# Layer 3's serial taps on the raw image, with scale and mean folded into the pointwise weights

## The chip, the core and the metric

The kernel runs as one program on one core of a Trainium2 chip. The metric is the time of one execution on the device in microseconds (us); the median of three runs before the change is 26167.87 us (26167.0 to 26171.33). The engines are called as in the profile: PE multiplies matrices, DVE works on vectors, ACT evaluates functions and scaled copies, POOL is a second vector engine, SP issues most transfers (DMA). Each engine works through its own queue in order.

## The reference, cut to what matters

The input x is 16 images of 192 channels and 64 x 64 points. Four layers follow one another, each of the form x = x + layer(group_norm(x)). The change concerns the last, and its group norm:

```python
# --- layer 3 --- (B, C, H, W) = (16, 192, 64, 64)
def _gn(v, G=32, eps=1e-5):            # groups of 6 channels
    g = v.reshape(B_, G, C_ // G, H_, W_)
    m = jnp.mean(g, axis=(2, 3, 4), keepdims=True)
    s = jnp.var(g, axis=(2, 3, 4), keepdims=True)
    return ((g - m) / jnp.sqrt(s + eps)).reshape(v.shape)

def _L3_conv_ref(x, w3, w5, wh, wv, pw, gamma, beta):   # x is already _gn(x)
    y = _dwconv(x, w3, 1) + _dwconv(x, w5, 2) + _dwconv(x, wh, (0, 3)) + _dwconv(x, wv, (3, 0))
    z = jnp.einsum('oc,bchw->bohw', pw, y)
    zn = (z - mean(z)) * jax.lax.rsqrt(var(z) + BN_EPS)     # over all images
    return jnp.clip(gamma * zn + beta, 0.0, 6.0)
x = x + _L3_conv_ref(_gn(x), ...)
```

The four depthwise convolutions (3x3, 5x5, 1x7 and 7x1, all with zeros outside the image) are one sum of 29 taps: the 25 points of the 5x5 square, the two ends of the 1x7 row and the two ends of the 7x1 column.

## The kernel before, in words

Two images make a pair: 384 channels, held as three tiles of 128 partitions (j = 0, 1, 2). There are 8 pairs, and `pair` runs for each the function `scans` and then `layer3`.

**scans** is layer 2 (a state-space scan) of the pair, 768 steps. Beside it runs a generator `fr` (`stream`), of which a few items are issued per scan step: layers 0 and 1 of the next pair, and at the end `ahead`, the depthwise convolution of layer 3 for tile j = 0 of the present pair. `ahead` works in 8 units of 512 points: 20 taps on PE (`a_p <- a_x,diag`), 6 on ACT and POOL (`a_g`, `a_m`), 3 on DVE; the sum is copied by ACT (`a_y`) and stored in `y0_d` by SP. The order of all engines is that of the program text (`keep_in_program_order`). At the end of `scans` (lines 1360 to 1365) the last four sums are added up on PE, `finish` takes the statistics of the last rows of the tile `X` (tile j = 2 of the layer's input, 70 x 70 with a border of zeros) and stores them, and what is left of `fr` is drained. In the last pair there is no next pair, and `fr` is done long before.

**layer3** (line 1513) convolves the tiles j = 1 (`xp1`, in the profile `xp`, loaded from `x3_d`) and j = 2 (`X`, still in place). It first asks on SP for `xp1`, the diagonal weights `diag`, the pointwise weights `pw` (they lie in a part of `Xt`), parts of `y0_d`, and `xn`, the first tile of the next pair's scan. Then it runs `group_norm` (means over partitions by small matmuls with `grp` into `gn_sum`), normalises both tiles in place on DVE (line 1544), in two parts, first the upper 19 rows, and `xn` too (line 1549). Then come 8 units u: four chunks c of 16 rows, each for j = 1 and 2. The 29 taps of a unit are shared out by the list `TAPS`: the first 7 go to PE (`products`, matmuls with diagonal weights into `l_p`), the next 9 to ACT, which multiplies, and POOL, which adds (`side`, tiles `l_g` and `l_m`), the other 13 to DVE. `add_side(u - 1)` adds `l_g` into `l_p` on PE; DVE then does the last tap of unit u - 1, which also writes the result (`l_y`, or a part of `Xt`), and twelve of unit u (`vector`). From u = 3 on the pointwise product `z` of a finished chunk is made on PE (`z_pe`), copied by ACT (`z_act`), its statistics taken by DVE (`z_dve`). The last chunk's `z` is made in the next pair's scans (`last_z`).

The queue order of one round u, which decides who waits for whom, is:

```python
products(u, 0)                  # 1654
products(u, 1)
add_side(u - 1)
...
last_tap(u - 1)                 # 1668
vector(u)
z_dve()
```

The program records most instructions from the helper at line 71, so that line stands beside nearly all of them, and tiles have to be told apart by name.

Of the kernel before, what the change touches and what calls it, by code (L numbers as in the profile page):

```python
# [11 lines left out]
F32 = mybir.dt.float32  # L12
# [10 lines left out]
P = 128  # L23
# [22 lines left out]

TAPS = [(3, 0), (3, 6), (0, 3), (6, 3)] + [(y, x) for y in range(1, 6) for x in range(1, 6)]
PE_TAPS = 7  # L50
GP_TAPS = 9


VECTOR_CHUNKS = 9
# [58 lines left out]
def conv_preact_kernel(ctx: ExitStack, tc: tile.TileContext, a: dict):  # L113
# [49 lines left out]
    dsk = load("dsk", [P, K, NT])  # L163
    b1c = load("b1c", [P, NT])
    wc = const.tile([P, NT, 7, 7], F32, name="wc")
    one_c = const.tile([P, 1], F32, name="one_c")
    minus_c = const.tile([P, 1], F32, name="minus_c")
    nc.vector.memset(one_c, 1.0)
# [72 lines left out]
    with tc.tile_pool(name="prep", bufs=1) as prep, tc.tile_pool(  # L241
# [118 lines left out]
        for part, w in (  # L360
            (wc[:, :, 2:5, 2:5], w3x3),
            (wc[:, :, 3, :], w1x7),
            (wc[:, :, :, 3], w7x1),
        ):
            nc.vector.tensor_tensor(part, part, w, ALU.add)
        for j in range(NT):
            diag = prep.tile([P, AHEAD_PE, P], F32, name="diag", tag="diag", bufs=1)
            many = PE_TAPS if j else AHEAD_PE
            for t, (ty, tx) in enumerate(TAPS[:many]):
                nc.gpsimd.tensor_scalar(  # L370
                    diag[:, t, :], ident, wc[:, j, ty, tx : tx + 1], None, ALU.mult
                )
            nc.sync.dma_start(out=diag_d[:, j, :many, :], in_=diag[:, :many, :])
# [44 lines left out]
    def normalise(eng, o, v, gm, rstd, j):  # L418
        eng.tensor_scalar(o, v, gm[:, j : j + 1], rstd[:, j : j + 1], ALU.subtract, ALU.mult)
# [668 lines left out]
        E.gps.tensor_tensor(image(du), image(delta), columns(xn)[:, : LC // HW, :], ALU.mult)  # L1088
        return xn, bp, delta, du

    def scans(i, o, p3, st3, begun, nxt, closing):

        E = _Engines(tc, True)
        with ExitStack() as es:
# [264 lines left out]
                    add_up(s - LATE)  # L1359
            for s in range(total - LATE, total):  # L1360
                add_up(s)
            for g in (finish(NT - 1, todo[-1][2] // LC), fr):
                for _ in g:
                    E.between()
            E.between()

    def ahead(i, E, ps, less, rstd):
# [89 lines left out]
    def end_z(E, i):  # L1457

        for j in range(NT):
            E.dve.bn_aggr(zmv[:, j, :], zst[:, j, :, :].rearrange("p c s -> p (c s)"))  # L1460
        E.sp.dma_start(out=zstat_d[i], in_=zmv.rearrange("p j s -> p (j s)"))
# [15 lines left out]
    def last_z(i):  # L1477

        def run(E, ps, pool):
            c = HW // 16 - 1  # L1480
            held, stats = None, []
            for jo in range(NT):
                for h in range(2):
                    for call in stats:
                        E.later(call)
                    stats.clear()
                    if held is not None:
                        held()
                    p = ps("cz_p")
                    z_product(E, p, jo, h, kept)  # L1490

                    def held(jo=jo, h=h, p=p):
                        z = pool.tile([P, 512], F32, name="cz", tag="cz", bufs=2)
                        E.act.copy(z, p)
                        stats.append(lambda: E.dve.bn_stats(zst[:, jo, 2 * c + h, :], z))
                        at = 1024 * c + 512 * h
                        E.sp.dma_start(out=row_tiles(z_d[i])[:, jo, at : at + 512], in_=z)

                    yield
            for call in stats:  # L1500
                E.later(call)
            stats.clear()
            held()
            yield
            for call in stats:
                E.later(call)
            yield
            E.later(lambda: end_z(E, i))
            yield

        return run

    def layer3(i, st3, o_next):
        E = _Engines(tc, True)
        units = [(c, j) for c in range(4) for j in range(1, NT)]
        own = PE_TAPS + GP_TAPS

        with tc.tile_pool(name="l3s", bufs=1) as stat, tc.tile_pool(name="l3y", bufs=2) as yk, tc.tile_pool(
            name="l3z", bufs=3
# [13 lines left out]
            E.sp.dma_start(out=xp1, in_=x3_d[i, 1])  # L1533
            E.sp.dma_start(out=diag, in_=diag_d[:, 1:, :PE_TAPS, :])
            E.sp.dma_start(out=pw, in_=a["pw"])
            for c in (0, 1, 3):
                load_y0(c)
            loaded = load_first(E, o_next) if o_next is not None else None
            xps = {1: xp1, 2: X}
            gm = stat.tile([P, NT], F32, name="gm")  # L1540
            rstd = stat.tile([P, NT], F32, name="rstd")
            for _ in group_norm(E, st3, stat, banks, gm, rstd, aside=False):
                pass
            for rows in (slice(3, 22), slice(22, 3 + HW)):
                for j in (1, 2):
                    v = xps[j][:, rows, inside]
                    normalise(E.dve, v, v, gm, rstd, j)
            if o_next is not None:
                normalise(E.dve, loaded[0], loaded[0], o_next.gm, o_next.rstd, 0)

            def window(j, c, rows, tap):
                return xps[j][:, c + tap[0] : c + tap[0] + rows, tap[1] : tap[1] + HW]
# [4 lines left out]
            def side(u, taps):  # L1557
                if u < len(units):
                    c, j = units[u]
                    for n in taps:  # L1560
                        tap = TAPS[PE_TAPS + n]
                        if n == 0:
                            m = gs[u] = wk.tile([P, 1024], F32, name="l3_g")
                        else:
                            m = wk.tile([P, 1024], F32, name="l3_m", bufs=3)
                        E.act.activation(
                            image(m), window(j, 16 * c, 16, tap), AF.Copy, scale=factor(j, tap)
                        )
                        if n:
                            E.gps.tensor_tensor(gs[u], gs[u], m, ALU.add)  # L1570

            def products(u, h):
                if u < len(units):
                    c, j = units[u]
                    if h == 0:
                        pss[u] = pt.tile([P, 1024], F32, name="l3_p")
                    cs = slice(512 * h, 512 * h + 512)
                    for t, tap in enumerate(TAPS[:PE_TAPS]):
                        E.pe.matmul(
                            pss[u][:, cs],  # L1580
                            diag[:, j - 1, t, :],
                            window(j, 16 * c + 8 * h, 8, tap),
                            start=(t == 0),
                            stop=(t == PE_TAPS - 1),
                        )

            def add_side(u):
# [21 lines left out]

            def vector(u):  # L1610
                if u < len(units):
                    for tap in TAPS[own:-1]:
                        tap_on_vector(u, tap, pss[u])

            def last_tap(u):
# [10 lines left out]
            def z_act(key):  # L1626
                c, jo, h = key
                if h == 0:
                    zs[c, jo] = zk.tile([P, 1024], F32, name="z")
                E.act.copy(zs[c, jo][:, 512 * h : 512 * h + 512], zps.pop(key))  # L1630
                stats.append(key)

            def z_dve():
# [8 lines left out]
            rounds = len(units) + (1 if o_next is not None else 3)  # L1642
            late, begun = [], None
            for u in range(rounds):
                c = (u - 3) // 2
                todo = [(c,) + x for x in halves[3 * ((u - 3) % 2) :][:3]] if u >= 3 else []
                side(u, range(0, 2))
                for key in late[:1]:
                    z_act(key)
                side(u, range(2, 4))  # L1650
                for key in late[1:]:
                    z_act(key)
                late = []
                products(u, 0)
                products(u, 1)
                add_side(u - 1)
                for key in todo[:2]:
                    z_pe(*key)
                side(u, range(4, 7))
                if todo:  # L1660
                    z_act(todo[0])
                side(u, range(7, GP_TAPS))
                if todo:
                    z_pe(*todo[2])
                    late = todo[1:]
                if u == 5 and o_next is not None:
                    begun = begin(E, o_next, loaded, lambda: pt.tile([P, 1024], F32, name="l3_p"))
                last_tap(u - 1)
                vector(u)
                z_dve()  # L1670
                if u == 4:
                    load_y0(2)
# [2 lines left out]
            z_dve()  # L1675
            if o_next is None:
                end_z(E, i)
            return begun

    def pair(i, q, more, begun, closing):  # L1680

        with tc.tile_pool(name="st3", bufs=1) as p3:
            st3 = p3.tile([P, NT, 8, 6], F32, name="st3")
            nxt = None if more is None else (more, sets[1 - q])
            scans(i, sets[q], p3, st3, begun, nxt, closing)
            if more is not None:
                return layer3(i, st3, sets[1 - q])
            with tc.tile_pool(name="zl", bufs=2) as pool:
                got = [load_z(u, pool) for u in range(3)]
                layer3(i, st3, None)  # L1690
                final(got, pool)

    def load_z(u, pool):
# [196 lines left out]
```

## Time and profile before

| what | value |
|---|---|
| median of 3 runs | 26167.87 us |
| time of the profiled execution | 26165.92 us |
| its span, first to last instruction | 26164.1 us |
| mean granted PE clock | 0.954 |
| DVE, 12 taps of a unit (`l_p<-X,wc,l_p`) | 15.86 us |
| POOL, mean of one add `l_g<-l_g,l_m` | 2406 ns |
| stretch 3965.2 to 4022.4 (first pair: end of the scans to the first DVE tap of layer 3) | DVE busy 19.69 of 57.20 us, PE 47.47, ACT 15.18, POOL 22.74 |
| stretch 4022.4 to 4190.0 (the rest of layer 3) | DVE busy 142.78 of 167.60 us, PE 144.33, ACT 82.24, POOL 143.64 |

A line of the timeline reads: start in us from the beginning of the span, length in us, engine, line of the program, operation, output <- inputs, shapes, count; and in brackets the time that the engine had been idle before, and what ended it. A matmul in f32 appears as two records, here called passes. A line of the table of groups ends in the busy time, the mean of one in ns, and the idle time before, with what ended it.

### The profile page before, as it was taken

The numbers are of one execution on the slowest core, as the hardware profiler recorded it, in microseconds if no ns is written. First come the engines' busy times: TensorE is split into PE (matmuls) and PEld (weight loads), VectorE is DVE, ScalarE is ACT, GpSimd is POOL, SyncE is SP. The second block draws the span as 40 slices with busy tenths as digits, with TensorE's granted clock in tenths as the row PEclk, the third lists the DMA queues.
The fourth block names the chain that finished last, engine by engine and source line by source line (L and its number), as shares of the span: only waits on it lengthen the run. The fifth ranks groups of instructions, "written<-read, shape, count | busy, mean of one in ns | idle before, by whom it ended". The sixth has DMA issues, their size and how long they took to land. (4 is left out here: it accounts for less than half of the span.)

```text
span 26164.1 us, 211030 instructions
## 1 busy us (share of the span) xinstructions
PE 23141.7 (88%) x58228; PEld 9496.0 (36%) x58228; DVE 23813.2 (91%) x15461; ACT 16268.9 (62%) x23559; POOL 20558.9 (79%) x10503
## 2 busy tenths in 40 slices
PE   7899989999899988999889998999989998866773
PEld 3344333433334333443334433343333433322231
DVE  7499998999899998999989999899989999899995
ACT  7388456874578655885558845687457865444443
POOL 3388877887788877888778887788778887777773
PEclk9899999999999999999999999999999999988896
DMA  3589875898678975899758987589867997567766
GB/s 84 155 227 229 222 227 169 228 225 223 196 200 230 227 221 168 225 233 225 223 167 228 227 223 226 169 229 226 223 189 205 229 227 222 160 187 193 196 200 270
DMA packets 2025599, 5449.12 MB, mean 208 GB/s; under 512 B 552616, under 2 KB 552840, under 8 KB 2007904
## 3 DMA queue, kind: packets, MB, share of 16 engines
q1 hardware_dynamic: 1799776, 4575.16, 60.2%
q0 software_dynamic: 221184, 805.40, 16.2%
q10 hardware_dynamic: 3456, 55.05, 0.5%
q8 instruction: 465, 7.62, 0.1%
q14 instruction: 718, 5.88, 0.1%
HBM read 3887.10 MB, written 358.39 MB: 162 GB/s over the span
## 5 line engine op out<-in xcount | busy, mean ns | idle before, releaser
L71 POOL TENSOR_TENSOR h<-h,cb 128x1024 f32<-128x1024 f32 x6144 | 14910.2, 2488 | 3330.5 <-ACT state L71 2798.7
L71 DVE TENSOR_TENSOR_SCAN h<-dA,state,pbt 128x1024 f32<-128x1024 f32 x4608 | 10806.5, 2345 | 541.9 <-ACT dA L71 91.4
L71 PE MATMUL ysum<-h,ident 128*128 128x512 f32 x18432 | 9050.3, 615 | 113.8 <-DMA h<-h 108.6
L71 DVE TENSOR_TENSOR pbt<-du,pbt 128x1024 f32<-128x1024 f32 x6144 | 7429.4, 1209 | 289.8 <-PE pbt L71 268.4
L71 ACT ACTIVATE dA<-delta,t_alog 128x1024 f32<-128x1024 f32 x6144 | 7036.6, 1146 | 6.6
L71 PEld LDWEIGHTS ysum<-h,ident 128*128 128x128 f32 x18432 | 3612.2, 197 | 4321.7 <-issue 3909.2
L71 ACT COPY state<-h 128x1 f32<-128x1 f32 x6144 | 1143.0, 186 | 5828.6 <-DVE h L71 5811.2
L71 DVE TENSOR_TENSOR_SCAN h<-dA,pbt 128x1024 f32<-128x1024 f32 x1536 | 3509.2, 2285 | 179.6 <-ACT dA L71 26.6
L71 PE MATMUL pbt<-bp,pick 96*128 96x512 bf16 x8192 | 2549.0, 394 | 1220.1 <-DVE h L71 1211.6
L71 PE MATMUL p<-m,wms 128*96 128x512 f32 (+1 forms) x5376 | 2664.7, 597 | 59.4 <-ACT lu L71 35.3
L71 PEld LDWEIGHTS <-pick 96*128 96x128 bf16 x8192 | 691.6, 100 | 4013.6 <-DVE h L71 2468.2
L71 PE MATMUL l_p<-l_xp,w1s 128*128 128x512 f32 x3920 | 1850.0, 593 | 0.0
L71 POOL DMA_DIRECT2D h<-h x1536 | 1356.2, 883 | 496.6 <-POOL h L71 427.0
L71 PE MATMUL pbt<-bp,pick_mix 96*128 96x512 bf16 x4096 | 1270.9, 392 | 516.7 <-DVE h L71 514.9
L71 ACT ACT_TABLE_LOAD x1103 | 1415.1, 1283 | 19.5
L71 PE MATMUL p<-t,wts 96*128 96x512 f32 x2688 | 1374.3, 592 | 0.0
L71 PE MATMUL p<-m,wts 96*128 96x512 f32 x2688 | 1302.3, 600 | 48.6 <-ACT m L71 44.4
L71 POOL TENSOR_TENSOR l_g<-l_g,l_m 128x1024 f32<-128x1024 f32 x512 | 1229.9, 2406 | 105.8 <-ACT l_m L71 71.9
L71 PEld LDWEIGHTS p<-m,wms 128*96 128x96 f32 (+1 forms) x5376 | 936.8, 177 | 834.5 <-issue 335.3
L71 PE MATMUL a_p<-a_x,diag 128*128 128x512 f32 x2560 | 1224.1, 600 | 1.4 <-ACT state L71 1.4
L71 ACT ACTIVATE m<-p,bias 96x512 f32<-96x512 f32 x1344 | 906.4, 674 | 488.8 <-PE p L71 487.9
L71 ACT ACTIVATE m<-m,bias,sp 96x512 f32<-96x512 f32 x1344 | 1077.9, 802 | 143.7 <-DMA m<-l_xn 136.4
(314 smaller groups left out, 21192.0 us busy)
## 6 DMA issues: line engine op xcount, KB each, us to landing
cb<-cp_d SPq DMA_DIRECT2D x2048, 512.0 KB
cb<-c_d SPq DMA_DIRECT2D x2048, 512.0 KB
h<-h POOLq DMA_DIRECT2D x1536, 512.0 KB, 7.2
cb<-cp_d SPq DMA_DIRECT2D x2048, 256.0 KB
cb<-c_d SPq DMA_DIRECT2D x2048, 256.0 KB
m<-l_xn SPq DMA_DIRECT2D x2928, 128.0 KB
bp<-bp_d SPq DMA_DIRECT2D x384, 192.0 KB
rl<-x_d ACTq DMA_DIRECT2D x24, 2240.0 KB
```

Of the source, the lines that this page charges most:

```text
L71: return self._tc.keep_in_program_order(call(*args, **kw))
```

## The change

The depthwise taps of the tiles j = 1 and 2 read the image as it is, not normalised. The border of both tiles is set to the group's mean instead of zero, so that a tap on it equals a tap on zero after the subtraction. As the convolution is linear, the scale 1/std of each channel goes into the rows of the pointwise weights `pw`, and the mean times the sum of the taps' weights (`wsum`), through `pw`, into a constant `zb` that is subtracted from `z` as a bias. The group norm is moved from `layer3` into the end of `scans`, ahead of the rest of `fr`, and two items of `fr` follow each of its steps. The taps are shared out in another order (the middle column first), unit 0 has 3 taps on PE and so 17 on DVE, the second chunk of rows comes first. The next pair's `xn` is normalised by ACT, in parts, during units 1 to 4. After the last unit POOL sets the border of `X` to zero again.

```diff
-TAPS = [(3, 0), (3, 6), (0, 3), (6, 3)] + [(y, x) for y in range(1, 6) for x in range(1, 6)]
+TAPS = [(y, 3) for y in range(7)] + [(3, 0), (3, 6)] + [(y, x) for x in (1, 2, 4, 5) for y in range(1, 6)]
 PE_TAPS = 7
 GP_TAPS = 9
+FIRST_PE = 3
+CHUNKS = (1, 0, 2, 3)
...
+        nc.vector.tensor_reduce(wsum, wc.rearrange("p j y x -> p j (y x)"), AX.X, ALU.add)
...
+    def pads(E, v, gm, j):
+
+        for to in (v[:, :3, :], v[:, 3 + HW :, :], v[:, inside, :3], v[:, inside, 3 + HW :]):
+            E.act.copy(to, gm[:, j : j + 1].unsqueeze(2).to_broadcast(list(to.shape)))
...
-            for g in (finish(NT - 1, todo[-1][2] // LC), fr):
-                for _ in g:
+            for _ in finish(NT - 1, todo[-1][2] // LC):
+                E.between()
+            E.between()
+            gn = group_norm(
+                E, st3, p3, lambda name: pb.tile([P, LC], F32, name="pbt"), gm3, rstd3, aside=False
+            )
+            for at, _ in enumerate(gn):
+                if at == 1:
+                    pads(E, X, gm3, NT - 1)
+                for _ in range(2):
+                    next(fr, None)
                     E.between()
+            for _ in fr:
+                E.between()
             E.between()
...
-                        E.act.copy(z, p)
+                        E.act.activation(z, p, AF.Identity, bias=zb[:, jo : jo + 1])
...
-        units = [(c, j) for c in range(4) for j in range(1, NT)]
-        own = PE_TAPS + GP_TAPS
+        units = [(c, j) for c in CHUNKS for j in range(1, NT)]
+
+        def many(u):
+            return PE_TAPS if u else FIRST_PE
...
-            for _ in group_norm(E, st3, stat, banks, gm, rstd, aside=False):
-                pass
-            for rows in (slice(3, 22), slice(22, 3 + HW)):
-                for j in (1, 2):
-                    v = xps[j][:, rows, inside]
-                    normalise(E.dve, v, v, gm, rstd, j)
+            pads(E, xp1, gm, 1)
+            gw = stat.tile([P, NT], F32, name="gw")
             if o_next is not None:
-                normalise(E.dve, loaded[0], loaded[0], o_next.gm, o_next.rstd, 0)
+                less = stat.tile([P, NT], F32, name="less")
+                E.act.activation(less, o_next.gm, AF.Copy, scale=-1.0)
+
+            def norm_first(n):
+                if o_next is not None and n < NC_:
+                    v = loaded[0][:, LC * n : LC * n + LC]
+                    on_scalar(E, v, v, less, o_next.rstd, 0)
+
+            def scale_pw():
+                for b, (ji, jo) in enumerate(BLOCKS):
+                    if ji:
+                        E.act.activation(pw[:, b, :], pw[:, b, :], AF.Copy, scale=rstd[:, ji : ji + 1])
+                E.dve.tensor_tensor(gw, gm, wsum, ALU.mult)
+
+            def constant():
+                p = banks("zp")
+                for jo in range(NT):
+                    into = [x for x in INTO[jo] if x[1]]
+                    for n, (b, ji) in enumerate(into):
+                        E.pe.matmul(p[:, jo : jo + 1], pw[:, b, :], gw[:, ji : ji + 1], ...)
+                E.act.activation(zb, p[:, :NT], AF.Copy, scale=-1.0)
...
-                    for t, tap in enumerate(TAPS[:PE_TAPS]):
+                    for t, tap in enumerate(TAPS[: many(u)]):
...
-                    for tap in TAPS[own:-1]:
+                    for tap in TAPS[many(u) + GP_TAPS : -1]:
...
-                E.act.copy(zs[c, jo][:, 512 * h : 512 * h + 512], zps.pop(key))
+                E.act.activation(
+                    zs[c, jo][:, 512 * h : 512 * h + 512], zps.pop(key), AF.Identity, bias=zb[:, jo : jo + 1]
+                )
...
                 add_side(u - 1)
+                if u == 2:
+                    constant()
...
                 side(u, range(7, GP_TAPS))
+                if u == 1:
+                    scale_pw()
+                norm_first(u - 1) if u else None
...
+            else:
+                for edge in (X[:, :3, :], X[:, 3 + HW :, :], X[:, inside, :3], X[:, inside, 3 + HW :]):
+                    E.gps.memset(edge, 0.0)
```

`on_scalar` is a pass that subtracts the mean and a pass that multiplies by the scale, both on ACT; `normalise` does both in one pass of the engine it is given.

## The prediction, made before the changed kernel ran

> **What bounds the kernel now.** I read the page first, for the engines, and then the table of groups kept apart by shape.
>
> ```profile
> PE 23141.7 (88%) x58228; PEld 9496.0 (36%) x58228; DVE 23813.2 (91%) x15461; ACT 16268.9 (62%) x23559; POOL 20558.9 (79%) x10503
> ```
>
> ```profile
> L71 DVE SCALAR_TENSOR_TENSOR l_p<-X,wc,l_p 128x1024 f32<-128x1024 f32 x384 | 495.1, 1289 | 12.3
> L71 DVE TENSOR_SCALAR X<-X,gm,rstd 128x2880 f32<-128x2880 f32 x8 | 30.3, 3785 | 0.0
> L71 DVE TENSOR_SCALAR xn<-xn,gm,rstd 128x4096 f32<-128x4096 f32 x7 | 22.6, 3233 | 41.4 <-DMA xn<-x_d 41.4
> ```
>
> DVE is busy 91% of the span, so DVE work that disappears looks like a gain. But a mean over the span says nothing of the few us where the change is made. The normalising passes (3785 and 3233 ns are the two largest) stand behind long waits, so I went to the timeline of the hand-over from scans to layer 3 in the first pair: PE alone, then DVE alone, and the load of `xp` from the whole timeline.
>
> ```profile
> 3965.82 7.03 PE L71 MATMUL ysum<-h,ident 128*128 128x512 f32 x16
> 3972.68 1.02 PE L71 MATMUL a_p<-a_g,ident 128*128 128x512 f32 x2
> 3973.54 17.54 PE L71 MATMUL a_p<-a_x,diag 128*128 128x512 f32 x40
> 3990.92 1.02 PE L71 MATMUL a_p<-a_g,ident 128*128 128x512 f32 x2
> 3995.88 3.12 PE L71 MATMUL gn_sum<-mean,t_grp 128*128 128x1 f32 x14 [3.93 <-DVE mean L71]
> 3999.91 3.15 PE L71 MATMUL gn_sum<-d,t_grp 128*128 128x1 f32 x14 [0.92 <-DVE d L71]
> 4007.94 14.47 PE L71 MATMUL l_p<-xp,diag 128*128 128x512 f32 x28 [4.89 <-DMA diag<-diag_d]
> 4022.25 12.32 PE L71 MATMUL l_p<-X,diag 128*128 128x512 f32 x28
> 4038.46 2.76 PE L71 MATMUL l_p<-l_g,ident 64*64 64x512 f32 x8 [3.89 <-DVE l_p L71]
> 4058.46 3.68 PE L71 MATMUL l_p<-l_g,ident 64*64 64x512 f32 x8 [4.06 <-DVE l_p L71]
> ```
>
> ```profile
> 3996.02 0.32 SPq L71 DMA_DIRECT2D xp<-x_d  x1
> ```
>
> ```profile
> 4005.66 0.94 DVE L71 TENSOR_SCALAR xp<-xp,gm,rstd 128x1216 f32<-128x1216 f32 x1 [2.41 <-DMA xp<-x_d]
> 4019.16 2.86 DVE L71 TENSOR_SCALAR xn<-xn,gm,rstd 128x4096 f32<-128x4096 f32 x1 [6.30 <-DMA xn<-x_d]
> 4022.45 15.87 DVE L71 SCALAR_TENSOR_TENSOR l_p<-xp,wc,l_p 128x1024 f32<-128x1024 f32 x12 [0.43 <-PE l_p L71]
> 4041.26 1.28 DVE L71 SCALAR_TENSOR_TENSOR l_y<-xp,wc,l_p 128x1024 f32<-128x1024 f32 x1 [2.95 <-PE l_p L71]
> 4042.46 15.86 DVE L71 SCALAR_TENSOR_TENSOR l_p<-X,wc,l_p 128x1024 f32<-128x1024 f32 x12
> ```
>
> Read it as a chain. After the last `ysum` PE is full without a gap from 3972.68 to 3991.94: the closing of one unit of `ahead` and all of the next. Three DVE taps, the copy `a_y` and its store follow, and only behind that store, in SP's queue, is `xp` asked for, at 3996.02. It has landed at 4005.66, `diag` behind it at about 4007.94, and then PE begins. **The group norm (3995.88 to 4004.20, when POOL's `rstd` ends) and the normalising of `xp` lie inside that load.** The other parts, to 4012.87, and `xn`, to 4022.02, lie beside the 14.47 us of unit 0 on PE. DVE's first tap waits for PE. From there each round is DVE's 15.86 us, `add_side`, the last tap, and so on. Late rounds come close to PE's bound (12.32 of products, 1.93 of sums, 6.28 of `z`, against a period of 20.2 to 20.9), but every round starts from the one before, so a start that is late by some us stays late to the end of layer 3. Seven hand-overs look alike: `xp` landed 2.2 to 2.5 us ahead of PE's first product in each. The eighth, in the last pair, has nothing left of `fr`, and loaded `xp` at 25122.2:
>
> ```profile
> 25586.12 1.69 PE L71 MATMUL gn_sum<-mean,t_grp 128*128 128x1 f32 x14 [3.48 <-DVE mean L71]
> 25588.66 3.15 PE L71 MATMUL gn_sum<-d,t_grp 128*128 128x1 f32 x14 [0.84 <-DVE d L71]
> ```
>
> **The change part by part**, for one of the seven hand-overs.
>
> *The group norm moves ahead of the rest of `fr`: +10.1 us.* PE works in order, so the first `gn_sum` now stands before the 44 passes of `ahead` and waits for the copy of `X` (1.03), the statistics (1.29) and the means (1.03). The last pair has just this order: 3.48 us of idle PE, where the row above goes on at once. The 14 passes of the first sum took 3.12, 2.56, 3.12, 3.12, 3.12, 3.00, 3.12 and 1.69 us in the eight pairs, 2.86 in the mean. After such gaps PE runs its first passes at half speed: the 28 passes of unit 0 took 14.47 us where 28 take 12.32 warm, 2.1 more; I charge the 2.1 to `ahead`. The second sum follows seven or so taps, warm: 1.69. Sum 3.48 + 2.86 + 2.1 + 1.69 = 10.1. Bounds: 3.48 + 1.69 + 1.69 = 6.9 if the clock holds, and 3.48 + 3.12 + 3.15 + 2.1 = 11.9. Everything behind shifts by this: DVE's three taps, `a_y`, the store, `xp`, `diag`. DVE's and POOL's small steps hide beside `ahead`; ACT stops for four copies into the border of `X`, which wait for the store of its last rows, but ACT had 15.64 us of idle time there before the last `a_y`. POOL's five adds of that unit (6.67 us) still fit beside PE.
>
> [...]
>
> *What it takes out of the wait for `xp`: 0.* The group norm, 0.94 of `xp` and 0.93 of `X` lay beside loads that stay; with them gone, `diag` still lands where it did. In their place come four ACT copies of about 200 elements into `xp`'s border: between 0.19 (128x1) and 0.57 (128x512) each, nearest to the 0.385 of a 128x128, about 1.6 us together and 0.8 to 2.3 at the bounds, inside the 2.3 between `xp` and `diag`. If that cover were gone, they would cost themselves. POOL's first add comes about 1 us later after the load than before, but needs only to be ready for `add_side`, with 8 x 2.41 = 19.3 us against 21 of DVE.
>
> *Unit 0 has 3 taps on PE: -7.0 us.* 12 passes instead of 28, so 16 x 0.435 fewer; the slow ones stay. *And 17 on DVE: +5.3.* 4 x 1.32 (15.86 / 12) before the first `add_side`. While DVE does them PE idles some 9 us instead of 3.89, and `add_side` costs 3.68 instead of 2.76, as in the next round: *+0.9* (bounds 0 and 0.9).
>
> *`xn` on ACT: 0.* DVE's pass ended before PE let DVE begin. The eight ACT passes of 1.13 go into units 1 to 4, where ACT spends 9 x 1.16 and at most 1.7 on `z` out of 20 us. *Scaling `pw`* (5 x 0.385) and *the constant* (10 passes of 0.12 to 0.22 in round 2, which has no `z` yet): 0, hidden by DVE's 15.86. *The bias in `z`'s copy:* 674 instead of 577 ns by ACT's row `m<-p,bias`, once at the tail: *+0.1*. *Zeroing the border of `X`*, four POOL memsets of about 0.33 (row `l_xp<-`), between the last tap at 4187.4 and POOL's next instruction at 4192.45: 0.
>
> Sum for a hand-over: 10.1 - 7.0 + 5.3 + 0.9 + 0.1 = **+9.4 us**; seven make +66. In the last pair no PE work is displaced: PE can start when the second sum ends, 25591.8 instead of 25594.14, so -2.3 - 7.0 + 5.3 + 0.9 + 0.1 = -3.0. But the border copies wait for the store of `X`, issued behind a 2 MB load, and can take back up to 5; I take -2. In all **+64 us**. The profiled execution has 26165.92 (span 26164.1 and 1.8 around it), so 26230; the median of the runs is 2 us above it, so 26232.
>
> **The rivals.**
>
> *The moved group norm costs nothing* (the wait is filled after all, or PE was not what ended the drain). For it: in 37.5 of the 57.2 us up to the first tap DVE is idle, so something could overlap. Against: PE's 44 passes without a gap. Then -7.0 + 5.3 + 0.9 + 0.1 = -0.7 each, -7 in all: 26161.
>
> *The loads run ahead* and the time falls. The place is SP's queue: if `xp` and `diag` were issued while `ahead` still computes, as in the last pair, products would begin when PE is free, at 3991.94 + 10.1 = 4002.0 instead of 4007.94: -5.9 - 7.0 + 5.3 + 0.9 + 0.1 = -6.6 each, -48 with the last pair; -70 with the low bound of 6.9. It decides from the point where the loads start 9.4 us ahead of where I put them. For it: the group norm and its tiles, which `layer3` had to wait for, are out of the way. Against: the order of SP's queue is unchanged, with the last `a_y` store in front. 26120.
>
> *ACT starves POOL* in units 1 to 4: POOL stands at 19.3 of 20 us, and if each 1.13 pass pushed its adds back and they came to end the round, 8 x 1.13 x 7 = 63 more: 26295. Against: three `l_m` buffers, and ACT idles 1.27 us before almost every `l_m`, waiting for POOL.
>
> **How the numbers follow.** What a measurement of this kernel can tell from no change is about 0.2%, 52 us. Forecast 0.70, group norm free 0.10, loads ahead 0.12, ACT starves POOL 0.08. The forecast's own range is 7 x (6.9 - 7.0 + 5.3) - 3 = +33 to 7 x (11.9 - 7.0 + 5.3 + 0.9 + 0.1) + 2 = +80, or 26201 to 26248; seven tenths of its chance lie above +52. So slower 0.70 x 0.7 + 0.08 = 0.57, faster about 0.07 (a good half of the loads ahead), the rest 0.36 within 0.2%. The range reaches down to the free group norm and a little above its own top: 26160 to 26255, leaving out the two rivals of 0.20.
>
> **What would show it.** Right: the first `gn_sum` about 3.5 us after `ysum`, `xp` asked for about 10 us later after `ysum` than before (23.2), 12 passes before DVE's first tap, 16 taps in a row, and layer 3 unchanged from there. Wrong: `xp` asked for before the last `a_y` store, PE's passes of `ahead` between `ysum` and `gn_sum`, or rounds that grow in units 1 to 4.

## The result, and the profile after

The changed kernel takes 26257.78 us in the median of seven runs (26249.62 to 26266.31); the kernel before takes 26167.0 beside it. The ratio is 1.0034, interval 1.0025 to 1.0044: slower, by 91 us. The prediction had said slower by 64, with a range that ended at 26255, 2.8 us too low.

The engines' line of the page of the changed kernel:

```profile
PE 23113.7 (88%) x58180; PEld 9468.0 (36%) x58180; DVE 23785.2 (91%) x15463; ACT 16383.7 (62%) x23734; POOL 20557.1 (78%) x10531
```

DVE is busy 28 us less than before (23813.2), because the normalising passes have gone and only four more taps per pair have come in. The kernel is 91 us longer all the same. The share of an engine tells nothing here. The order at the hand-over does.

PE alone at the first hand-over of the changed kernel, from the last `ysum` on (the helper now stands at line 73):

```profile
3965.95 7.03 PE L73 MATMUL ysum<-h,ident 128*128 128x512 f32 x16
3976.78 2.44 PE L73 MATMUL pbt<-mean,t_grp 128*128 128x1 f32 x14 [3.79 <-DVE mean L73]
3979.08 2.05 PE L73 MATMUL a_p<-a_g,ident 128*128 128x512 f32 x2
3980.93 8.82 PE L73 MATMUL a_p<-a_x,diag 128*128 128x512 f32 x16
3989.59 1.62 PE L73 MATMUL pbt<-d,t_grp 128*128 128x1 f32 x14
3991.06 10.63 PE L73 MATMUL a_p<-a_x,diag 128*128 128x512 f32 x24
4001.53 1.02 PE L73 MATMUL a_p<-a_g,ident 128*128 128x512 f32 x2
4018.66 7.06 PE L73 MATMUL l_p<-xp,diag 128*128 128x512 f32 x12 [16.11 <-DMA diag<-diag_d]
4047.29 3.68 PE L73 MATMUL l_p<-l_g,ident 64*64 64x512 f32 x8 [9.30 <-DVE l_p L73]
```

The load of `xp` in SP's timeline of the same stretch:

```profile
4006.63 0.32 SPq L73 DMA_DIRECT2D xp<-x_d  x1
```

DVE's first taps:

```profile
4025.91 21.23 DVE L73 SCALAR_TENSOR_TENSOR l_p<-xp,wc,l_p 128x1024 f32<-128x1024 f32 x16 [20.52 <-ACT l_m L73]
4051.01 1.28 DVE L73 SCALAR_TENSOR_TENSOR l_y<-xp,wc,l_p 128x1024 f32<-128x1024 f32 x1 [2.06 <-PE l_p L73]
```

PE now stands idle for 3.79 us for the means, does the first sum (named `pbt` here) in 2.44, and is slow after it: 2.05 for two passes that take 1.02 when warm, 8.82 for 16 where 40 took 17.54 before, so 2.8 us lost. The 44 passes of `ahead` end at 4002.55 instead of 3991.94. So the store of `a_y`, and `xp` behind it, come 10.6 us later, and PE waits 16.11 us for `diag`. The bracket of DVE's first taps names ACT's `l_m`, which ended at 4025.87; but PE's 12th product ended at 4025.72, and in all seven hand-overs the first tap comes 0.2 us after that product, while ACT's piece had ended 0.5 to 1.7 us before it in the other six. DVE waits for PE there, as before.

All seven hand-overs, counted from the end of the last `ysum` (means, us):

| mark | before | after | moved | predicted |
|---|---|---|---|---|
| `xp` asked for on SP | 23.10 | 33.40 | +10.3 | +10.1 |
| PE's first product | 35.09 | 45.62 | +10.5 | +10.1 |
| DVE's first tap | 49.85 | 53.62 | +3.8 | +3.1 |
| first last tap | 68.79 | 78.61 | +9.8 | +9.3 |
| first scan of the next pair | 223.54 | 234.38 | +10.8 | +9.4 |

Seven times the last row is 75.9. In this pair of traces the last pair gives back 3.1, and the scans, which the prediction took as unchanged, add 22.6: 75.9 + 22.6 - 3.1 + 0.1 is the whole difference of the two profiled executions, 95.5. The forecast had 66 for the hand-overs, nothing for the scans and -2 for the last pair.

Most of the scans' part sits at their start. PE alone, around the end of layer 3 and the first steps of the next scans, in the first hand-over of the kernel before (rows of `pbt` that stand between are left out here, in the next rows and in those of e9):

```profile
4182.40 3.68 PE L71 MATMUL l_p<-l_g,ident 64*64 64x512 f32 x8 [11.04 <-DVE l_p L71]
4186.02 6.35 PE L71 MATMUL zp<-l_y,Xt 128*128 128x512 f32 x14
4198.30 1.03 PE L71 MATMUL pbt<-bp,pick 96*128 96x512 bf16 x2 [5.06 <-DVE h L71]
4199.12 3.62 PE L71 MATMUL cz_p<-Xt 128*128 128x512 f32 x4
4202.53 1.97 PE L71 MATMUL gn_sum<-mean,t_grp 128*128 128x1 f32 x14
4204.80 1.88 PE L71 MATMUL cz_p<-Xt 128*128 128x512 f32 x4
```

The same place in the changed kernel, third hand-over:

```profile
10426.61 3.68 PE L73 MATMUL l_p<-l_g,ident 64*64 64x512 f32 x8 [11.04 <-DVE l_p L73]
10430.22 7.20 PE L73 MATMUL zp<-l_y,Xt 128*128 128x512 f32 x14
10443.34 1.03 PE L73 MATMUL pbt<-bp,pick 96*128 96x512 bf16 x2 [5.05 <-DVE h L73]
10444.16 3.62 PE L73 MATMUL cz_p<-Xt 128*128 128x512 f32 x4
10447.58 2.99 PE L73 MATMUL gn_sum<-mean,t_grp 128*128 128x1 f32 x14
10451.23 3.62 PE L73 MATMUL cz_p<-Xt 128*128 128x512 f32 x4
```

The instructions and the idle times are the same (11.04, 5.06 against 5.05), and the durations are not: the 14 products of `z` take 7.20 instead of 6.35, and after the second gap PE stays at half speed for longer, so that the second four products of `cz` also take 3.62 instead of 1.88. The profile's record of the granted clock says the same directly:

| stretch | PE busy | granted clock |
|---|---|---|
| before, first hand-over, 4196.5 to 4203.3 | 5.00 of 6.80 us | 0.50 |
| before, the next 6.8 us | 6.80 | 1.00 |
| changed, third hand-over, 10442.4 to 10449.2 | 5.86 of 6.80 us | 0.50 |
| changed, the next 6.8 us | 6.80 | 0.50 |

DVE then waits for `pbt` in the changed kernel:

```profile
10451.48 1.23 DVE L73 TENSOR_TENSOR pbt<-du,pbt 128x1024 f32<-128x1024 f32 x1 [0.44 <-PE pbt L73]
```

The first ten steps of the scans take about 42.3 us when PE recovers early (6.8 us at half clock) and 45 to 48 when it recovers late (13.7 us). In the kernel before one pair of six was of the late kind, in the changed one four, with two in between. (The seventh hand-over is left out: its ten steps take 37.9 us in every kernel.) By step 32 this is 17.9 of the 22.6. The other 4.7 are not explained, and needn't be: behind step 32 the scans of the 14 traces differ by up to 27 us in all, with the change and without.

### The profile page after: what moved, and what is told of

It is laid out like the page before. It is cut to its first block, busy times and chain, and to the rows that moved or that the text cites. A ratio compares the mean times of both kernels' runs of the same rounds, so it can differ in the third digit from the quotient of the medians.

```text
span 26259.7 us, 211130 instructions
## 1 busy us (share of the span) xinstructions
PE 23113.7 (88%) x58180; PEld 9468.0 (36%) x58180; DVE 23785.2 (91%) x15463; ACT 16383.7 (62%) x23734; POOL 20557.1 (78%) x10531
```

## The experiments

The kernel before, measured again beside these runs, has medians of 26166 to 26171. The columns are means of the marks above; "ten steps" is the sum of the first ten scan steps over six pairs, in the profiled execution.

| kernel | median (runs) | ratio to before | `xp` asked | first tap | hand-over | ten steps |
|---|---|---|---|---|---|---|
| before | 26167.0 (7) | | 23.10 | 49.85 | 223.54 | 257.6 |
| changed | 26257.78 (7) | 1.0034 | 33.40 | 53.62 | 234.38 | 274.4 |
| e1_gn_after | 26194.26 (11) | 1.001 | 23.10 | 43.08 | 224.78 | 271.6 |
| e2_gn_later | 26207.76 (11) | 1.0016 | 26.23 | 46.18 | 226.77 | 273.5 |
| e3_no_xn | 26254.47 (5) | 1.0034 | 33.34 | 52.94 | 234.09 | 274.4 |
| e4_first7 | 26271.06 (5) | 1.0042 | 33.62 | 60.55 | 236.36 | 273.2 |
| e5_before_taps | 26170.59 (11) | 1.0 | 23.10 | 50.01 | 223.93 | 263.3 |
| e6_before_bias | 26168.93 (11) | 1.0 | 23.10 | 50.20 | 224.52 | 261.6 |
| e7_loads_ahead | 26135.75 (11) | 0.9987 | 12.67 | 35.16 | 216.38 | 271.5 |
| e8_loads_gn_later | 26088.59 (6) | 0.9969 | 6.39 | 27.66 | 209.08 | 278.2 |
| e9_after_warm | 26231.58 (10) | 1.0025 | 33.84 | 54.28 | 232.69 | 269.9 |
| e10_best_warm | 26071.44 (5) | 0.9964 | 6.40 | 27.66 | 206.08 | 271.8 |
| e11_before_warm | 26166.24 (11) | 0.9998 | 23.10 | 49.71 | 221.86 | 263.0 |
| e12_no_bias | 26262.78 (5) | 1.0033 | 33.45 | 53.74 | 233.96 | 271.5 |

### Where the group norm stands

**e1_gn_after**: the changed kernel with the group norm behind the rest of `fr`, as before (the copies into the border of `X` move with it).

```diff
+            for _ in fr:
+                E.between()
+            E.between()
             gn = group_norm(...)
             for at, _ in enumerate(gn):
                 if at == 1:
                     pads(E, X, gm3, NT - 1)
-                for _ in range(2):
-                    next(fr, None)
-                    E.between()
-            for _ in fr:
-                E.between()
```

> The changed kernel, with the group norm put back behind the rest of the stream (the border copies of X move with it). Theory (the moved group norm lengthens PE's drain): xp is asked for 23.2 us after the last ysum again instead of 33.6, the group norm lies beside that load, and DVE's first tap comes at about 43 us instead of 53.5; the hand-over is about 10 us shorter than in the changed kernel, 7 x 10 = 70 less: about 26185, and 26165 if the scans' extra 20 us go too. Rival (17 taps on DVE, the border copies and the shifted work on ACT are what costs): the drain doesn't matter, at most 15 us less, 26240 or more.

It came out at 26194.26, ratio 1.001 (1.0001 to 1.0019), 63.5 us below the changed kernel. Its load is asked for where the kernel before asks, while the group norm's sums lie beside it. SP in its first hand-over:

```profile
3994.40 0.32 SPq L73 DMA_DIRECT2D xp<-x_d  x1
```

PE there:

```profile
3989.31 1.02 PE L73 MATMUL a_p<-a_g,ident 128*128 128x512 f32 x2
3994.26 3.12 PE L73 MATMUL pbt<-mean,t_grp 128*128 128x1 f32 x14 [3.93 <-DVE mean L73]
3998.32 3.12 PE L73 MATMUL pbt<-d,t_grp 128*128 128x1 f32 x14 [0.93 <-DVE d L73]
4006.11 7.75 PE L73 MATMUL l_p<-xp,diag 128*128 128x512 f32 x12 [4.68 <-DMA Xt<-in_pw]
```

The same idle 3.9 us and slow sums are there; nothing behind them is late by them. The sum of the hand-overs falls by 67.2 of the 75.9. So the moved group norm, with its border copies, is the main cause. Its ten steps stay at 271.6: the place of the group norm is not what slows the scans' start.

**e2_gn_later**: five items of `fr` are issued before the group norm, so that PE has work while the statistics are made; two items still follow each step.

```diff
+            for _ in range(5):
+                next(fr, None)
+                E.between()
             gn = group_norm(...)
```

> The changed kernel, with five items of the stream issued between the last rows' statistics and the group norm, so that PE has work while the means are made; the number of PE passes is the same. Theory: the idle 3.8 us before the first sum, its slow clock (1.2) and the slow passes behind it (2.1) go, the two sums of 1.65 each stay: xp asked for at about 26.5 us after the last ysum instead of 33.6, 7 less in each of seven hand-overs, about 26208. Rival (the passes themselves or their order cost, the wait doesn't): within 10 us of the changed kernel, 26250.

26207.76 (1.0007 to 1.0025), where the forecast was 26208. `xp` is asked for 3.1 us later than in the kernel before, about what two sums of 1.6 us cost on a warm PE: the idle time and the half speed, some 7 of the 10 us, have gone, the sums themselves remain. In its first hand-over PE is busy without a gap from 3969.4 to 3990.0 at a granted clock of 1.00, and each sum takes 1.62; in the changed kernel the clock was 0.53 from 3977.1 to 3984.0.

### Where the loads stand

**e7_loads_ahead**: in the changed kernel the last store of `a_y` is issued on ACT's queue instead of SP's, and `layer3` opens the space for `xp1` and `diag` first.

```diff
-                E.sp.dma_start(out=y0_d[i][:, 512 * u : 512 * u + 512], in_=y)
+                (E.act if u == 7 else E.sp).dma_start(out=y0_d[i][:, 512 * u : 512 * u + 512], in_=y)
...
-        with tc.tile_pool(name="l3s", bufs=1) as stat, ...
+        with tc.tile_pool(name="l3x", bufs=1) as xk, tc.tile_pool(name="l3s", bufs=1) as stat, ...
```

> The changed kernel, with the store of the last y0 part on ACT's queue and layer 3's pool for xp and diag put first, so that SP can ask for xp while PE still works on the stream. Theory (the loads hang behind that store, so all that lengthens the drain delays them): xp is asked for within some 5 us of the last ysum instead of 33.6, PE's first product comes when the drain ends, about 30 us after ysum instead of 45.7, DVE's first tap at 37.5 instead of 53; 15 less in each of seven hand-overs, 26150, or 26190 if ACT and POOL, which start only 10 us earlier, hold DVE up. Rival (the loads wait for memory that the stream still uses): nothing moves, 26258.

26135.75, ratio 0.9987 (0.9979 to 0.9996): 122 us faster than the changed kernel. The load is asked for while PE still works on `ahead`, and PE goes from `ahead` to layer 3 without a gap. It is asked for 12.67 us after `ysum`, not within the 5 that were expected: the store of the unit before (3980.00 in the first hand-over) still stands in SP's queue, and `xp` follows at 3980.68. The run doesn't tell the two edits apart, the store's queue and the order of the spaces.

**e8_loads_gn_later**: both edits, e2 and e7.

> Both edits together: five items of the stream before the group norm, and the loads free of the last store. Theory: the drain itself is now the bound and is 7 us shorter, DVE's first tap about 30 us after ysum; 22 less in each hand-over than the changed kernel, 26105, which is below the kernel before. Rival (once the loads are early, the place of the group norm doesn't matter, since ACT and POOL bound unit 0): as with the loads alone.

26088.59, ratio 0.9969 (0.9958 to 0.9981), 78 us faster than the kernel before. PE in its first hand-over, from the last `ysum` on:

```profile
3962.95 7.03 PE L73 MATMUL ysum<-h,ident 128*128 128x512 f32 x16
3969.82 1.02 PE L73 MATMUL a_p<-a_g,ident 128*128 128x512 f32 x2
3970.67 8.88 PE L73 MATMUL a_p<-a_x,diag 128*128 128x512 f32 x20
3979.40 1.61 PE L73 MATMUL pbt<-mean,t_grp 128*128 128x1 f32 x14
3980.88 6.33 PE L73 MATMUL a_p<-a_x,diag 128*128 128x512 f32 x14
3987.04 1.62 PE L73 MATMUL pbt<-d,t_grp 128*128 128x1 f32 x14
3988.52 2.82 PE L73 MATMUL a_p<-a_x,diag 128*128 128x512 f32 x6
3991.18 1.02 PE L73 MATMUL a_p<-a_g,ident 128*128 128x512 f32 x2
3992.03 5.42 PE L73 MATMUL l_p<-xp,diag 128*128 128x512 f32 x12
```

No brackets: PE never waits here. Both sums are quick, and the 12 products take 5.42 instead of 7.06. DVE's first tap comes 27.66 us after `ysum` instead of 53.62. Behind it `add_side` (at 4019.35) ends an idle time of 9.64 us and waits for POOL's `l_g`, no longer for DVE. One price is visible: in the last pair DVE's first tap moves from 17.9 to 32.0 us after `ysum`, as there `xp` had been asked for 461 us ahead of `ysum`'s end and is now asked for 2.3 us behind it; the last pair as a whole is 14 us longer. It is the same in e7. Whether the kernel before gains as much from earlier loads was not tried; its group norm and normalising passes would then no longer be hidden.

### The smaller terms

**e4_first7**: unit 0 with 7 taps on PE and 13 on DVE again (`FIRST_PE = 7`).

> The changed kernel with 7 taps on PE in unit 0 as in the other units (13 on DVE). By the prediction's terms PE's passes cost +7.0 and DVE's taps -5.3, add_side is warm again -0.9: +0.8 in each of eight, +6, 26264. Rival 1 (DVE's four taps are hidden somewhere): +7 each, 26310. Rival 2 (PE's passes are hidden): -6 each, 26210.

26271.06, with an interval of 1.0029 to 1.0056. The first tap comes 6.9 us later than in the changed kernel (predicted 7.0), the first last tap 1.4 later, the hand-over 2.0. By these marks three taps on PE are a small gain, 2.0 a hand-over where the sum of -7.0, +5.3 and +0.9 had 0.8. The total times alone don't tell the two kernels apart: the intervals overlap.

**e3_no_xn**: the eight passes of `norm_first` left out, so that the next pair's scan starts from a tile that is not normalised.

> The changed kernel without the eight ACT passes that normalise xn in units 1 to 4; it leaves out that normalisation, so the first tile of the following pair's scan is the raw one. My prediction charged these passes at 0: then 26258. Rival, from the trace after: in round 3 PE waits 1.8 us for a copy of z that ACT makes late, behind these passes; then that wait goes and each hand-over is about 1.3 us shorter, 9 less, 26249.

26254.47 against 26257.78: not told apart. The wait that the rival names, of 1.7 to 2.0 us ahead of a product of `z` in round 3 (`zp` at 4096.69 in the changed kernel), stands in three of the changed kernel's seven hand-overs and in five of the seven without the passes. So the passes don't make it, and the rival is wrong; what does make it is open. The mean hand-over is 234.09 against 234.38. In the rounds behind it PE runs without a gap in the first hand-over of both, and DVE waits 1.5 to 2.8 us for PE in each round.

### The start of the scans

**e5_before_taps**: the kernel before with the new order of `TAPS` alone. **e6_before_bias**: the kernel before with the copies of `z` and `cz` made with a bias, which is zero.

> The kernel before with only the new order of the taps. The scans of the changed kernel took 20 us longer in all than those before, which my prediction had at 0. Theory A (the order of taps makes PE's passes of the stream and of the units slower, 604 instead of 600 ns a record): +10 to +20, 26180 to 26190. Theory B (the clock's phase, or the bias): 26170.

> The kernel before with only the new form of z's copies, a bias of zeros in layer 3 and in the last z at the start of the next scans (674 instead of 570 ns each). Theory A (these copies hold up the first steps of the scans): the first 32 steps grow by 0.5 to 3 us in each of seven, +5 to +20. Theory B (PE's clock stays low for longer, by its phase): 26170, and the first 32 steps as before.

Ratio 1.0 in both (0.9991 to 1.0009, and to 1.0008). Neither edit alone makes the scans slow: ten steps at 263.3 and 261.6. Two pairs of six are of the late kind in each.

**e9_after_warm**, **e11_before_warm**, **e10_best_warm**: the changed kernel, the kernel before and e8, each with spare matmuls in the two gaps of PE that the rows above show.

```diff
+                if u == len(units) and o_next is not None:
+                    spare = pt.tile([P, 1024], F32, name="l3_p")
+                    for t in range(11):
+                        E.pe.matmul(spare[:, :512], diag[:, 1, t % 7, :], window(2, 48, 8, TAPS[t % 7]), ...)
                 add_side(u - 1)
...
                 spread(s)
+            if i:
+                spare = ps("warm")
+                for _ in range(5):
+                    E.pe.matmul(spare, pw[:, 0, :], kept[0][:, :512], ...)
```

> The changed kernel with 11 spare matmuls on PE in the last round of layer 3 (in the 11.04 us in which PE idles ahead of its last add_side) and 5 more in the 5 us gap at the start of the next scans; their sums go to a spare bank that nobody reads. Theory: the 17 us that the scans lost are PE's clock. In pairs where the products of z after the last tap took 7.2 us instead of 6.28, the first steps of the scans took 3.6 to 5.5 us more. Then the last add_side falls from 3.68 to about 1.93 (7 x 1.75 = 12 us), the tail loses its slow 1 us in four pairs (4), and the scans their 17: about 26225, and no pair has steps of 4.47, 4.27, 4.7, 4.5, 4.45 at its start. Rival: the scans' loss is not PE's clock; then only the 12 of add_side go: 26246. If the spare matmuls themselves delay the sums behind them, it is slower than 26258.

> The same spare matmuls in the kernel before. Its trace has one pair of six with slow first steps, so there is less to win: 12 from add_side, 1 from the tail, 4 from the first steps, about 26150. By the theory of the clock the two kernels with spare matmuls then differ by the hand-over alone, 70 to 76 us, not by 90; by the rival they still differ by 90.

> The best kernel so far (loads ahead of the store, group norm later; 26089) with the same spare matmuls. Its trace has five of six pairs with slow first steps, 21.8 us in all by step 32. By the theory of the clock 12 + 5 + 20 = 37 less: 26052. By the rival 12 less: 26077.

PE in e9, at the end of layer 3 of the first pair:

```profile
4181.46 9.79 PE L73 MATMUL l_p<-X,diag 128*128 128x512 f32 x22
4192.67 1.93 PE L73 MATMUL l_p<-l_g,ident 64*64 64x512 f32 x8 [1.41 <-DVE l_p L73]
4194.53 6.28 PE L73 MATMUL zp<-l_y,Xt 128*128 128x512 f32 x14
4201.58 4.56 PE L73 MATMUL warm<-Xt 128*128 128x512 f32 x10
4207.34 1.88 PE L73 MATMUL cz_p<-Xt 128*128 128x512 f32 x4
4209.06 1.62 PE L73 MATMUL gn_sum<-mean,t_grp 128*128 128x1 f32 x14
4212.98 3.53 PE L73 MATMUL cz_p<-Xt 128*128 128x512 f32 x4 [1.26 <-ACT x_gm L73]
```

With work in the gap `add_side` falls from 3.68 to 1.93, the products of `z` are at 6.28, the first `cz` at 1.88 and the sum at 1.62, at a granted clock of 1.00 from 4190 to 4211. So these rows were slow by PE's clock and nothing else. The sums of the hand-overs fall by 11.9 in e9 and 11.8 in e11, where 12 were expected for `add_side` and up to 4 for the tail. From the first last tap to the next scan both kernels now need 153.4 us, where the changed kernel had needed 155.77 and the kernel before 154.75. So the tail of e9 gave all that was expected, 16.5 in seven hand-overs; the stretch ahead of it is 0.7 us longer in e9, which is not explained.

But a second stretch of half speed follows a few us on (3.53 above, behind a wait of 1.26), and the ten steps improve only from 274.4 to 269.9 in e9 and grow from 257.6 to 263.0 in e11. The medians: 26231.58 (forecast 26225), 26166.24 (26150) and 26071.44 (26052). The changed kernel gains 26 us. The kernel before gains 5, which its interval (0.9989 to 1.0007) doesn't tell from nothing. The two now differ by 65 instead of 91, which looks like the theory of the clock (70 to 76) against the rival (90). In the two traces it is partly luck: the hand-overs differ by 75.8, the first 32 steps still by 7.0, the last pair by -3.6, and -13.9 come from the later steps of the scans, where neither the theory nor the rival expected anything. What the traces do show is that the difference over the first 32 steps shrinks from 17.9 to 7.0. All three gains are smaller than forecast, since the second stretch was not foreseen. e10 is the fastest kernel of the study, 0.9964 (0.9951 to 0.9978); its interval overlaps that of e8.

**e12_no_bias**: the changed kernel with plain copies of `z` and `cz`.

> The changed kernel with the plain copy of z and cz in place of the copy with a bias, so the constant is left out of z. The copy takes 0.58 instead of 0.69 us. If this longer copy in both places is what makes the start of the scans slow, the time falls by most of the 17: about 26241. If it is where PE's clock happens to stand when layer 3 ends, it stays within 10 us of the changed kernel: 26248 to 26266.

26262.78, four late pairs of six, ten steps at 271.5. The longer copy is not the cause on its own.

## Why the prediction was wrong, step by step

**The moved group norm**, +10.1: right. Measured +10.3 at `xp` and +10.5 at PE's first product, with the parts near the terms: 3.80 of idle time, 2.56 and 1.62 for the sums and 2.3 for the half-speed passes, in the mean of the seven, against 3.48, 2.86, 1.69 and 2.1. So the total is not a lucky one. e1 takes nearly all of it back, e2 shows that the idle time and the half speed are most of it.

**The 12 passes and the 17 taps**, -7.0, +5.3 and +0.9: right. In e1, where the group norm is out of the way, DVE's first tap is 6.8 us earlier than before and the first last tap 0.8 earlier; the sum said 7.0 and 0.8.

**`xn` on ACT, scaling `pw`, the constant: 0**. Right for `xn`, by e3; scaling `pw` and the constant were not taken out. From the first last tap to the next scan the changed kernel needs 155.77 us and the kernel before 154.75; the sum had 0.1 for this stretch. With spare matmuls in the last round the two need 153.41 and 153.38, so this 1 us a hand-over is PE's clock in the tail: the products of `z` are slow in five of the changed kernel's seven hand-overs and in one of those before. The other 0.5 us by which the hand-overs grew beyond the sum lie ahead of the first last tap and are open.

**"Layer 3 unchanged from there", and a sum that ended at the first scan: this failed.** The prediction put the scans at nothing because no line of theirs that matters was edited. They cost 22.6 in the two traces, of which 17.9 lie in the first 32 steps. Over all kernels without the change the ten steps are 257.6 to 263.3, over those with it and without spare matmuls 271.5 to 278.2, so some 13 of the 91 us belong to them. The tail's 1 us a hand-over, 7 in all, has the same cause. With either of the two gone the time would have lain inside the range, though near its upper end.

The cause is the clock that PE is granted. In the traces of the kernel before and of the changed kernel, the half clock behind the second gap lasts 13.65 us in all five late pairs, 6.83 in all five early ones; in the two between, a further 3.41 us of it come 16.9 and 16.8 us after the first scan. In both traces every stretch of one clock lasts a whole multiple of 3.4133 us, to within 0.013 us (650 stretches before, 644 after). Which kind comes up goes with the place where the half clock behind the gap begins: 1.1 to 1.6 us after the first scan in the late pairs, 0.0 to 0.6 us after it in the early ones, 0.15 and 0.26 us ahead of it in those between. (The seventh hand-over has 6.83 us in both, also in the changed kernel, where the half clock begins 1.15 us after the first scan.) The late kind shows from the third step on, which takes 4.47 or 4.48 us in the late pairs of the two traces and 3.92 in the others.

What remains open is why the change moves the first scan against the points where the clock changes, so that the late kind comes up in 5 of 18 pairs without it (early in 12) and in 34 of 48 with it (early in 7). The order of the taps, the bias, the group norm's place, `xn` on ACT and the first unit are each excluded as the sole cause (e5, e6 and e12, e1, e3, e4). The raw image, the border fills, the scaling of `pw` and the order of the chunks were not tried.

**The rivals.** "Costs nothing" (26161) fell with the marks. "ACT starves POOL" (26295) fell with e3, which removed the passes and gained 3 us that the noise covers. "The loads run ahead" was false of the change, as SP's order kept the store in front, but its mechanism was right, and its price for a hand-over: made true in e7, the first scan came 7.2 us earlier than in the kernel before, where the rival had 6.6. The total, 26135.75 against 26120, is higher by what the rival left out, some 11 us in the last pair and 14 in the first 32 steps of the scans.

## What to carry to other kernels

A small step that waits for other engines is free where a load hides it, as the group norm was before, and costs its wait, its own time and the half-speed work behind it when it is put ahead of a full queue: here 3.80, 4.18 and 2.3 us. Before moving it, look at what the queue must still do before the next load can start. Where an in-order queue holds a store that waits for its result in front of an independent load, try that order first: the store on another queue and the loads' space opened first were 122 us together, more than the whole change moved. And a sum of terms must run on to the point where the two traces are in step again: work that was not edited can change its time when it starts in another state of the clock, as the first ten steps of the scans did, from 257.6 us over six pairs to 274.4.

## What the runs showed of the hardware

Equal instructions after equal gaps ran at two speeds on PE: in the traces of the kernel before and of the changed kernel, 14 passes took 6.3 to 6.4 us in eight hand-overs and 6.9 to 7.4 us in six, after the same 11.04 or 11.05 us of idle time. Where the clock changes at the first scan is not left to chance in these traces. Counted back from there in steps of 3.413 us, the next such point after the end of `ysum` is 0.2 to 3.2 us away, anywhere in the 3.4, while at the first scan the half clock begins, in all 14 hand-overs, between 0.3 us ahead of it and 1.6 us after it. Something between the two seems to bring the kernel into step with these points; what does was not tried.

Keeping PE busy with sums that nobody reads brought 26 us in the changed kernel, and in the kernel before and in e8 5 and 17, which the intervals don't tell from nothing. It moved the half-speed stretch to the next gap rather than removing it: in e9 the first four passes of `cz` take 1.88 us and the next four, behind a wait of 1.26, 3.53.
